# First residuals queued ahead of the third and fourth right factor, and the last quarter finished and stored in two halves

## The chip, the cores and the metric

The kernel runs on one core of one Trainium2 chip. The metric is the device time of one execution in microseconds (us); lower is better. Every time below comes from the kernel's runs or from the trace of one profiled execution.

The core's engines run side by side and meet only at semaphores: TensorE (PE in the profile, its weight loads PEld), VectorE (DVE), ScalarE (ACT) and GpSimd (POOL). SyncE (SP) only issues transfers here. ACT and POOL can issue transfers too. Each engine works through its own instructions in order; an instruction that waits holds back everything behind it on that engine.

## The reference, cut to what matters

`x` has 64 sequences of 64 heads with 1024 features each. All of it is float32.

```python
y   = ssm_conv(x, itok, log_dt, C, ...)       # per head a causal convolution, cut at each sequence's length
s   = y @ Wr.T                                # 64 scores per token (a token is a sequence and a head)
G   = softmax over the 16 highest scores, 0 elsewhere
h   = einsum('nd,krd->nkr', y, A)             # 64 experts of rank 16: 1024 hidden values per token
out = x + 2 * einsum('nkr,kdr->nd', h * G[:, :, None], B)
```

Seen by TensorE, the last two lines are two products of a 1024 x 1024 matrix with 4096 tokens of 1024 values, with a gate between them and the residual `x` added at the end.

## The kernel before, in words

**Tiling.** The 64 heads are cut into 8 groups of 8 heads; with 64 sequences a group has 512 tokens, and its two halves have 256 each (`HT`). A matrix of 1024 features is 8 blocks of 128 partitions.

**First stage (up to 654.3 us).** For each group the convolution (`conv`), the gates (`gates`, `spread_gates`) and the first product (`first`, `seven`) run interleaved. The first product is cut into 2 x 2 blocks and made with seven block products in place of eight. The seven right factors are `y`'s blocks and sums of them; three of those sums stand in tiles of the pool `tq` (called `ty` in the trace). The gated result is written to memory as `hg_dram`, again as the seven right factors that the second product wants. The tile pools `gp`, `tq` and `hp` belong to this stage and are closed before `second` begins.

**Second stage (`second`, from 654.3 us).** It is cut by seven at two levels. The outer list `todo` has 28 entries `(sg, n)`: a pair `sg` of groups, and the outer product `n` in the order 1, 6, 7, 2, 5, 4, 3. The index in this list is `q`. Each entry makes seven inner products with `product(i)` in the order 1, 6, 7, 2, 5, 4, 3. `product(2, c11)` continues to sum in the accumulation bank (PSUM) of `product(1)`, and `product(3, c12)` in that of `product(5)`. Each inner product is two row halves (`ii`) of two matmuls each; in the trace a matmul of float32 counts as two, so that a product is eight rows of 128x256.

- `load_factor(sg, n, halves)` queues the right factor of an entry on SP, 512 KB for each of two groups. `places(q)` says where it goes: for `q % 4` of 2 and 3 it is the tile `qy`, which takes the room of one of the two `y` tiles of the first stage.
- `second_sums` (line 782) makes four sums out of a right factor on DVE (L788 in the trace). `second_level` (line 764) does the same to the left factor the first time that it is used (L771).
- `residuals(sg, m, s)` queues four tiles `o` of `x` on SP, 256 KB each, for one quarter of the output. The pools `op` that hold them lie where `gp`, `tq` and `hp` were.
- `parts_of(sg, n)` says what happens to the inner products. `ahead` and `early` give work on SBUF alone to POOL (`gt_`, line 811, L812 in the trace); `late` adds a bank to its place on DVE (`bank_into`, line 825, and `tt`, L307). `A` is the accumulator `acc_a`. For `n == 6` `ahead` adds the four quarters of `A` to the four tiles `o` of the first residuals, then `early` changes `A` itself.
- `stored` queues the finished 256 KB tile of a quarter on SP (`queued`).

The order on SP is the order in which it is written (`queued` keeps it). The order on DVE and PE is the framework's, by its own estimates, within what is pinned. In `second`, before the loop, the kernel before queues the right factors of `q` 2 and 3 and then the first residuals:

```python
for q in (2, 3):
    r_of[q] = places(q)
    load_factor(*todo[q], r_of[q])
residuals(0, 0, 0)
```

Of the kernel before, what the change touches and what calls it, by code (L numbers as in the profile page):

```python
# [55 lines left out]
NG = NH // HG  # L56
# [4 lines left out]
HT = TOK // NS2  # L61
# [31 lines left out]
def body(ctx: ExitStack, tc, x, xo, lens, par, dvec, at, bm, wt, cst, out):  # L93
    nc = tc.nc
# [266 lines left out]
    s, q = parts  # L361
# [432 lines left out]
    def second(places, rooms, loaded, next_loaded, made, second_level_of, spare, pools):  # L794

        op, ps, A, B = pools
        todo = [(sg, n) for sg in range(NG // 2) for n in (1, 6, 7, 2, 5, 4, 3)]
        outs, loads = {}, [0]  # L800

        def residuals(sg, m, s):
            room = op[loads[0] % len(op)]
            loads[0] += 1
            for a in range(2):
                for gg in range(2):
                    o = room.tile([P, 2, HT], F32, tag="o", name=f"o_{sg}_{m}{s}{a}{gg}")
                    queued(o.rearrange("p i t -> p (i t)"), xo[2 * sg + gg, m, s, a])
                    outs[m, s, a, gg] = o

        def gt_(o, a, b, op_):
            tc.keep_in_program_order(G.tensor_tensor(out=o, in0=a, in1=b, op=op_))  # L812

        PLACES = ((0, 0), (1, 1), (1, 0), (0, 1))
        SIGN = {(0, 0): 1, (0, 1): 1, (1, 0): 1, (1, 1): -1}
        LEFT = {(0, 1): 1, (1, 0): -1, (1, 1): -1}

        def add(engine, o, a, b, plus):
            engine(o, a, b, ALU.add if plus > 0 else ALU.subtract)

        def left_into(o, a, place, v, sign):

            add(gt_, o, a, v, sign * LEFT[place])

        def bank_into(o, place, bank, sign):
            add(tt, o, o, bank, sign * SIGN[place])

        def whole(o, place, bank, v):
            if place == (0, 0):
                nc.scalar.copy(o, bank)  # L830
            elif place == (1, 1):
                stt(o, v, -1.0, ALU.mult, bank, ALU.subtract)
            else:
                add(tt, o, bank, v, LEFT[place])

        def parts_of(sg, n):


            def nothing(*_):
                pass  # L840

            def into(o, sign):
                def early(place, v):
                    left_into(o[place], o[place], place, v, sign)

                def late(place, bank, v):
                    bank_into(o[place], place, bank, sign)
                return early, late

            def out_(m, s):  # L850
                return {p: outs[(m, s) + p] for p in PLACES}

            def stored(m, s, late):
                o = out_(m, s)

                def late_(place, bank, v):
                    late(place, bank, v)
                    queued(out[(2 * sg + place[1], m, s, place[0])],
                           o[place].rearrange("p i t -> p (i t)"))
                return late_  # L860

            def all_of(o, a, op_):
                def ahead():
                    for p in PLACES:
                        gt_(o[p], o[p], a[p], op_)
                return ahead

            if n == 1:
                return nothing, nothing, lambda place, bank, v: whole(A[place], place, bank, v)
            if n == 6:  # L870
                return (all_of(out_(0, 0), A, ALU.add),) + into(A, -1)
            if n == 2:
                early, late = into(out_(0, 0), 1)
                return all_of(out_(1, 1), B, ALU.subtract), early, stored(0, 0, late)
            if n == 7:
                def early(place, v):
                    left_into(B[place], A[place], place, v, 1)

                def late(place, bank, v):
                    add(tt, B[place], A[place] if v is None else B[place], bank, SIGN[place])  # L880
                return nothing, early, late
            if n == 5:
                o = out_(1, 1)

                def late(place, bank, v):
                    if v is None:
                        bank_into(A[place], place, bank, 1)
                        bank_into(o[place], place, bank, -1)
                    else:
                        m = spare[2 if place == (1, 0) else 5]  # L890
                        whole(m, place, bank, v)
                        gt_(A[place], A[place], m, ALU.add)
                        tt(o[place], o[place], m, ALU.subtract)
                return all_of(out_(1, 0), B, ALU.subtract), nothing, stored(1, 1, late)
            m, s = (1, 0) if n == 4 else (0, 1)
            early, late = into(out_(m, s), 1)
            return all_of(out_(0, 1), A, ALU.add) if n == 3 else nothing, early, stored(m, s, late)


        behind = {1: (1, 1), 6: (1, 0), 2: (0, 1)}  # L900
        sums, r_of = {0: loaded}, {1: next_loaded}
        for q in (2, 3):
            r_of[q] = places(q)
            load_factor(*todo[q], r_of[q])
        residuals(0, 0, 0)
        _, *now = parts_of(*todo[0])
        for q, (sg, n) in enumerate(todo):
            if q + 1 < len(todo):
                steps = second_sums(r_of.pop(q + 1), *rooms(q + 1))
            else:  # L910
                steps = iter(())

            def ahead_step():
                next(later, None)
                try:
                    next(steps)
                except StopIteration as e:
                    if e.value is not None:
                        sums[q + 1] = e.value

            right_ = sums.pop(q)
            left_ = made[n]
            early, late = now
            later = second_level_of(todo[q + 3][1]) if q + 3 < 7 else iter(())

            def product(i, bank=None, more=False):
                first = bank is None
                if first:
                    banks, t = (ps, "ps") if more else (ps_f, "pf")
                    bank = banks.tile([P, 2, HT], F32, tag=t, name=f"s{sg}_{n}_{i}")  # L930
                for ii in range(2):
                    for k in range(2):
                        nc.tensor.matmul(  # L933
                            bank[:, ii, :], lhsT=left_[i - 1][:, k, ii * P : (ii + 1) * P],
                            rhs=right_[i - 1][:, k, :],
                            start=(first and ii == 0 and k == 0),
                            stop=(ii == 1 and k == 1 and not more),
                            skip_group_check=True,
                        )
                return bank  # L940

            def new(t, i):
                return fp.tile([P, 2, HT], F32, tag=t, name=f"{t}{i}_{sg}_{n}")

            c11 = product(1, more=True)
            p1 = new("p", 1)
            nc.scalar.copy(p1, c11)  # L947
            p6 = product(6)
            v2 = new("u2", 2)
            tt(v2, p1, p6, ALU.subtract)  # L950
            early((0, 1), v2)
            ahead_step()
            p7 = product(7)
            v3 = new("u3", 3)
            tt(v3, p7, v2, ALU.add)
            early((1, 1), v3)
            early((1, 0), v3)
            if q == 0:
                sum_factors()
            product(2, c11)  # L960
            late((0, 0), c11, None)
            ahead_step()
            c12 = product(5, more=True)
            late((1, 1), c12, v3)
            ahead_step()
            p4 = product(4)
            late((1, 0), p4, v3)
            ahead_step()
            product(3, c12)
            late((0, 1), c12, v2)  # L970
            ahead_step()
            if q + 1 < len(todo):
                ahead, *now = parts_of(*todo[q + 1])
                ahead()
            if n in behind:
                residuals(sg, *behind[n])
            elif n == 4 and sg + 1 < NG // 2:
                residuals(sg + 1, 0, 0)
            if q + 4 < len(todo):
                r_of[q + 4] = places(q + 4)  # L980
                load_factor(*todo[q + 4], r_of[q + 4])
# [90 lines left out]
    for _ in products:  # L1072
# [3 lines left out]
        if n in (5, 6):  # L1076
            i = (1, 6)[n - 5]
# [77 lines left out]
```

## Time and profile before

| | us |
|---|---|
| three runs | 1003.79, 1004.41, 1004.69 (median 1004.41) |
| profiled execution, its own time | 1004.42 |
| its span in the trace | 1002.6 |
| time outside the span | 1.82 |
| PE busy | 985.1 (98% of the span) |
| DVE busy | 717.5 (72%) |
| POOL busy | 330.8 (33%) |
| ACT busy | 165.8 (17%) |
| mean DMA rate | 140 GB/s |

A timeline row has the start in us, the duration in us, the engine, the line, the operation, the tile written and the tiles read, the shape and the count. Rows of equal work that follow each other are merged. A bracket gives the idle time before the row and what ended it. PE's rows overlap by about 0.17 us, since a matmul's end is modelled. In the answers on waits, a row has who waited, for whom, the total in us, the number of waits and the longest. PEclk is the TensorE clock that was granted, as a share of full speed.

### The profile page before, as it was taken

To read this page: it belongs to the slowest core of one execution; us is meant where nothing else is said; L and a number is where in the kernel's file an instruction comes from. 1 tells how busy PE (TensorE), PEld (TensorE's weight loads), DVE (VectorE), ACT (ScalarE), POOL (GpSimd) and SP (SyncE) were. 2 spreads that over 40 slices of the span, in tenths; PEclk is the share of its full clock that TensorE was granted. 3 is DMA by queue.
4 is the path that set the end of the run, shared out by engine and by line. 5 is a ranking of instruction groups with operands and counts; after the bars stand their busy time and mean duration, and the time that the engine had idled before them with its cause. 6 is when DMAs were issued, how large, how long until landed. Compare 5 with 4: busy or idle time off the path is not lost.

```text
span 1002.6 us, 12158 instructions
## 1 busy us (share of the span) xinstructions
PE 985.1 (98%) x4416; PEld 738.4 (74%) x4416; DVE 717.5 (72%) x1672; ACT 165.8 (17%) x339; POOL 330.8 (33%) x278
## 2 busy tenths in 40 slices
PE   7999999999999999999999999998999999999998
PEld 3367666686676676677677578887888888888887
DVE  6887778587587587676646649778965786686674
ACT  5436041131141041031001100000000000000000
POOL 0002023122123113114103202245655673654555
PEclk9999999999999999999999999999999999999999
DMA  7113316315405315315315154473474367267432
GB/s 273 64 53 112 126 42 184 137 52 154 137 22 184 118 40 163 137 43 163 115 65 158 48 198 163 158 272 137 158 264 167 126 211 271 85 210 253 132 119 105
DMA packets 66189, 140.86 MB, mean 140 GB/s; under 512 B 9362, under 2 KB 17874, under 8 KB 66130
## 3 DMA queue, kind: packets, MB, share of 16 engines
q1 hardware_dynamic: 49376, 94.54, 27.4%
q0 software_dynamic: 15744, 44.07, 14.0%
q10 hardware_dynamic: 1010, 1.48, 0.6%
q8 instruction: 35, 0.57, 0.2%
q14 instruction: 24, 0.20, 0.1%
HBM read 92.79 MB, written 47.25 MB: 140 GB/s over the span
## 4 chain that ended last, share of the span: by engine, by line
PE 96%; DVE 3%; DMA 1%; issue 0%; SPq 0%; DVEq 0%
PE h L502 38%; PE s L933 33%; PE pc L581 6%; PE pc L587 5%; PE pu L555 5%; PE psh L640 3%; PE sum L190 2%; PE pb L277 1%; DMA waa<-in_at 1%; PE psc L649 1%; PE pb L279 1%; DVE t L788 0%; DVE y L593 0%; PE pg L685 0%; PE pk L292 0%
## 5 line engine op out<-in xcount | busy, mean ns | idle before, releaser
L318 DVE SCALAR_TENSOR_TENSOR s<-s,turn 128x64 f32<-128x64 f32 (+1 forms) x576 | 146.0, 303 | 36.7 <-ACT s L560 30.2
L502 PE MATMUL h<-y,waa 128*128 128x256 f32 x512 | 122.7, 384 | 0.0
L502 PE MATMUL h<-y,was 128*128 128x256 f32 x512 | 117.8, 381 | 0.0
L502 PE MATMUL h<-ty,was 128*128 128x256 f32 x512 | 116.4, 380 | 0.0
L502 PEld LDWEIGHTS h<-y,waa 128*128 128x128 f32 x512 | 93.7, 190 | 27.0 <-issue 15.4
L502 PEld LDWEIGHTS h<-y,was 128*128 128x128 f32 x512 | 96.1, 190 | 19.9 <-issue 7.5
L502 PEld LDWEIGHTS h<-ty,was 128*128 128x128 f32 x512 | 96.6, 190 | 16.7 <-issue 3.9
L719 POOL TENSOR_TENSOR hg<-h_p,gx 128x512 f32<-128x512 f32 x16 | 26.8, 1678 | 223.1 <-DVE h_p L318 215.4
L719 POOL TENSOR_TENSOR hg<-h_u,gx 128x512 f32<-128x512 f32 x32 | 49.5, 1546 | 136.2 <-DVE h_u L307 136.1
L593 DVE TENSOR_TENSOR y<-pc,mask 128x512 f32<-128x512 f32 x64 | 42.5, 684 | 37.0 <-PE pc L587 37.0
L947 ACT COPY p<-s 128x512 f32<-128x512 f32 x28 | 16.4, 586 | 317.4 <-PE s L933 317.4
L696 POOL DMA_DIRECT2D gx<-gt_dram x56 | 33.5, 625 | 97.2 <-DMA gt_dram<-gt 90.3
L812 POOL TENSOR_TENSOR o<-o,acc_a 128x512 f32<-128x512 f32 x32 | 48.5, 1535 | 47.8 <-ACT acc_a L830 21.7
L581 PE MATMUL pc<-x,toep 128*128 128x512 f32 x128 | 62.0, 607 | 0.0
L502 PE MATMUL h<-ty,waa 128*128 128x256 f32 x256 | 58.8, 382 | 0.0
L307 DVE TENSOR_TENSOR hg<-hg 128x512 f32<-128x512 f32 x64 | 42.8, 689 | 21.4 <-POOL hg L719 20.5
L560 ACT COPY s<-pu 128x448 f32<-128x448 f32 x64 | 33.9, 532 | 140.8 <-PE pu L555 140.4
L587 PE MATMUL pc<-s,w 64*128 64x448 f32 x256 | 56.8, 562 | 0.0
L502 PEld LDWEIGHTS h<-ty,waa 128*128 128x128 f32 x256 | 47.9, 190 | 10.7 <-issue 4.6
L555 PE MATMUL pu<-x,bt 128*64 128x448 f32 x256 | 55.5, 553 | 0.0
L812 POOL TENSOR_TENSOR o<-o,b_room 128x512 f32<-128x512 f32 x32 | 49.9, 1580 | 9.8 <-DVE b_room L307 9.8
L307 DVE TENSOR_TENSOR o<-o,s 128x512 f32<-128x512 f32 x52 | 35.4, 681 | 23.6 <-PE s L933 18.5
(225 smaller groups left out, 1627.8 us busy)
## 6 DMA issues: line engine op xcount, KB each, us to landing
x<-in_x SPq DMA_DIRECT2D x32, 512.0 KB
hg_dram<-hg POOLq DMA_DIRECT2D x16, 1024.0 KB, 6.0
o<-in_xo SPq DMA_DIRECT2D x64, 256.0 KB
out<-o SPq DMA_DIRECT2D x64, 256.0 KB
gx<-gt_dram POOLq DMA_DIRECT2D x56, 256.0 KB, 6.6
qy<-hg_dram SPq DMA_DIRECT2D x28, 512.0 KB
r<-hg_dram SPq DMA_DIRECT2D x26, 512.0 KB
hg_dram<-hg POOLq DMA_DIRECT2D x16, 768.0 KB, 4.4
```

Source lines behind the costliest of these rows:

```text
L307: V.tensor_tensor(out=o, in0=a, in1=b, op=o_)
L318: V.scalar_tensor_tensor(out=o, in0=a, scalar=s, in1=b, op0=o1, op1=o2)
L502: nc.tensor.matmul(bank[:, ii, :], lhsT=fac[n - 1][:, k, (j + ii) * P : (j + ii + 1) * P], rhs=rf[n - 1][:, k, :], start=(first and ii == ...
L555: nc.tensor.matmul(pu[hh * NS : (hh + 1) * NS, :], lhsT=bt[:, i, (1 - c) * P + hh * NS : (1 - c) * P + (hh + 1) * NS], rhs=xt[:, hh, : NCH ...
L560: nc.scalar.copy(s[:, c], pu.rearrange("p (k b) -> p k b", b=NB))
L581: nc.tensor.matmul(pc, lhsT=toep[:, 2 * i + hh, :], rhs=xt[:, hh, :], start=True, stop=False)
L587: nc.tensor.matmul(pcs[hh][:, NB:], lhsT=w[o : o + NS, c, i, 1:], rhs=s[o : o + NS, c].rearrange("p k b -> p (k b)"), start=False, stop=(c ...
L593: marks["y"] = V.tensor_tensor(out=y[:, :, :, 2 * i + hh, :], in0=pcs[hh].rearrange("p (k s b) -> p k s b", s=NS2, b=HB), in1=mask.rearran ...
L696: i = queue.dma_start(gx[:, ii, :], gt_dram[g, c * n : (c + 1) * n, :].unsqueeze(1).to_broadcast([n, RANK, TOK]),)
L719: G.tensor_tensor(out=o, in0=a, in1=b, op=op)
L812: tc.keep_in_program_order(G.tensor_tensor(out=o, in0=a, in1=b, op=op_))
L933: nc.tensor.matmul(bank[:, ii, :], lhsT=left_[i - 1][:, k, ii * P : (ii + 1) * P], rhs=right_[i - 1][:, k, :], start=(first and ii == 0 an ...
```

## The change

The first residuals are queued ahead of the right factors of `q` 2 and 3. And in the last entry of the list, the last inner product is made by its two row halves: each is added to its half of the output tile and stored by itself, the first half through SP, the second through ACT's queue.

```diff
+        def last_out(product, bank):
+            sg, o = NG // 2 - 1, outs[0, 1, 0, 1]
+            for ii in range(2):
+                product(3, bank, rows=(ii,))
+                bank_into(o[:, ii], (0, 1), bank[:, ii], 1)
+                (queued, scalar_queued)[ii](
+                    out[2 * sg + 1, 0, 1, 0][:, ii * HT : (ii + 1) * HT], o[:, ii])
+
+        def scalar_queued(o, i):
+            tc.keep_in_program_order(nc.scalar.dma_start(o, i))
...
+        residuals(0, 0, 0)
         for q in (2, 3):
             r_of[q] = places(q)
             load_factor(*todo[q], r_of[q])
-        residuals(0, 0, 0)
...
-            def product(i, bank=None, more=False):
+            def product(i, bank=None, more=False, rows=(0, 1)):
...
-                for ii in range(2):
+                for ii in rows:
...
-            product(3, c12)
-            late((0, 1), c12, v2)
+            if q + 1 < len(todo):
+                product(3, c12)
+                late((0, 1), c12, v2)
+            else:
+                last_out(product, c12)
```

## The prediction

> **What bounds the kernel now.** I read the page's chain of work first, then PE's waits from 640 us on, then the timeline around the one large wait, then SP's issues and the DMA rate ahead of it, and last the final 6 us. The chain that ended last:
>
> ```profile
> PE 96%; DVE 3%; DMA 1%; issue 0%; SPq 0%; DVEq 0%
> ```
>
> PE sets the end, so only what PE waits for, and what follows its last matmul, is worth anything. In the second stage PE waited twice:
>
> ```profile
> PE s L933 <- DVE acc_a L307: 3.2, 1, 3.2
> PE s L933 <- DVE o L307: 0.4, 1, 0.4
> ```
>
> From entry 4 on (708.56) to the last product (996.92) PE makes 167 products in 288.36 us, 1.727 each, with no gap. By that step the second product of entry 2, fifteen after 654.32, was due at 680.22. It starts at 685.40: **5.18 us are lost in entry 1**, and another 0.71 in entry 3. The timeline of the first:
>
> ```profile
> 665.87 1.26 POOL L812 TENSOR_TENSOR o<-o,acc_a 128x512 f32<-128x512 f32 x1 [3.17 <-DMA o<-in_xo]
> ...
> 670.13 0.69 DVE L307 TENSOR_TENSOR u<-p,s 128x512 f32<-128x512 f32 x1 [0.91 <-PE s L933]
> ...
> 670.51 4.61 POOL L812 TENSOR_TENSOR o<-o,acc_a 128x512 f32<-128x512 f32 x3 [3.38 <-DMA o<-in_xo]
> 670.74 1.58 DVE L771 TENSOR_TENSOR e<-wbs 128x512 f32<-128x512 f32 x1
> ...
> 675.20 5.05 POOL L812 TENSOR_TENSOR acc_a<-acc_a,u 128x512 f32<-128x512 f32 x3
> ...
> 675.72 1.75 DVE L788 TENSOR_TENSOR t<-qy 128x512 f32<-128x512 f32 x1
> ...
> 677.50 1.64 DVE L788 TENSOR_TENSOR t<-qy,t 128x512 f32<-128x512 f32 x1
> 679.06 1.74 DVE L788 TENSOR_TENSOR qy<-qy 128x512 f32<-128x512 f32 x1
> 680.73 0.67 DVE L307 TENSOR_TENSOR acc_a<-acc_a,s 128x512 f32<-128x512 f32 x1
> ...
> 681.46 3.46 PE L933 MATMUL s<-b_room,ey 128*128 128x256 f32 x8 [3.23 <-DVE acc_a L307]
> ...
> 684.71 0.86 PE L933 MATMUL s<-qy,wbs 128*128 128x256 f32 x2
> 685.40 1.89 PE L933 MATMUL s<-ey,e 128*128 128x256 f32 x8
> ```
>
> Read backwards: `product(3, c12)` may not write its bank before DVE has read it (680.73). That read stands in DVE's order behind three sums of `qy`, stretched from 0.68 to 1.7 us by POOL. POOL is late because its four adds into the first residuals waited for those to land, at 665.8 and 670.5. Of the 5.18 us, 3.23 are idle time and 1.78 slow matmuls: the next ten rows take 3.94 us, not 2.16. SP's issues, and the DMA share and GB/s (the last two columns) ahead of that:
>
> ```profile
> 644.15 0.80 SPq L776 DMA_DIRECT2D b_room<-hg_dram  x2
> 654.51 1.75 SPq L776 DMA_DIRECT2D qy<-hg_dram  x4
> 656.30 15.67 SPq L776 DMA_DIRECT2D o<-in_xo  x8
> ```
>
> ```profile
> 652.00:654.00 2.00, 2.00 (x11) 1.77 (x10) 1.97 (x3) 0.00 (x0) 1.53 (x1) 1.00 0.00 0
> ...
> 658.00:660.00 2.00, 2.00 (x11) 1.77 (x10) 1.93 (x4) 0.00 (x0) 0.55 (x1) 1.00 1.07 416
> ```
>
> The DMA engines stand idle until 655.3 because SP waits for PE's last use of `y`, whose room `qy` takes; then they are full, and the residuals are last in line. The end:
>
> ```profile
> 996.92 1.89 PE L933 MATMUL s<-qy,e 128*128 128x256 f32 x8
> ...
> 998.85 0.69 DVE L307 TENSOR_TENSOR o<-o,s 128x512 f32<-128x512 f32 x1 [0.98 <-PE s L933]
> ```
>
> DVE ends at 999.54; the store and the end of the program take 3.06 us more.
>
> **What the Trainium skill says.** (1) "SBUF — State Buffer", section "SBUF: two separate sides": a DVE operation with two SBUF inputs and a POOL operation that reads SBUF exclude each other for the whole instruction. The trace agrees to 0.1 us: POOL 1.26 alone, DVE 0.68 alone, but 1.6 to 1.75 where they meet, while DVE operations that read a bank stay at 0.68 beside a busy POOL. (2) "TensorE: Matmul & The Clock Gate", section "Part 1: The HAM clock gate": after an idle window of about 3.4 us TensorE runs at half clock until a busy window has passed. The trace agrees: PEclk 0.50 from 682 to 685 after 3.23 us idle; after a gap of 1.38 us before 55.87 it was not (1.00). (3) "PSUM — Partial Sum Buffer", section "PSUM bank collisions raise a hardware error": accesses must be kept apart by bank, not by address. That bears on the split tail.
>
> **Part 1: residuals first.** Moved on SP: four issues of 256 KB past four of 512 KB. Nothing is added or removed. In the built program the first residual waits only for the inner product that reads `tq`'s last sum, the last but one of the first stage, done at 651.0; `qy` keeps its own wait (654.5). So:
> - Residuals: issue 651.1, data 0.8 us later (as `qy`: 654.51 to 655.3), 1.05 MB at 416 GB/s 2.5 us, completion at most 1.5 (as at the end of the trace): landed by about 655.9. Had they waited as long as `qy`, 659.3, which would still do.
> - `qy`: 0 to 2.5 us later than before, where its first sum ran at 667.21. With the 0.79 MB store of `hg` in between, 3.9 MB at 416 from 655.3 is 664.7, with completion 666. First use is now 671.35. Hidden. The second `hg` store and the loads behind it gain from the idle time used.
> - POOL's four adds then wait for ACT and DVE alone: after POOL's store issue (ends 662.7) they run 662.7 to 668.7, beside DVE work that reads banks. Before they ended at 675.1.
>
> The built order on DVE also changes: in entry 1 the sums of `qy` are spread between the other work. Three sums of `qy` leave the free stretch from 667.2 to 669.2 and come after `u`; between `u` (670.13) and the bank read that PE needs there are six sums with two SBUF inputs, as before, but beside them POOL has three adds where it had six. I walk it with the lock rule: DVE alone 0.60 a step back to back, after POOL its end + 0.57; POOL 1.13 once it has the lock. On the old order this gives 672.3, 674.0, 677.5, 679.1 and 680.8 for the stretched sums' ends, as the trace has. New order: u 670.82; e 671.42; POOL `acc_a` 672.55; ey 673.12; u3 673.73; ey 674.33; POOL 675.46; qy 676.03; POOL 677.16; meanwhile `acc_a` (first bank) 676.63; e 677.73; t 678.33; **`acc_a` (the wanted bank) 678.93**. PE goes on at 679.0 in place of the due 676.77: 2.23 us lost, not 5.18. After it DVE catches up by 683.7, ahead of the next bank at 684.4, and from there order and distances are those of before, the 0.71 of entry 3 included. **Gain 2.95.** Bounds: no lock at all, acc_a at 676.6, all 5.18; three POOL operations each in full (3.4) and the clock gated again (1.8), about 0.
>
> **Part 2: the tail.** Two matmul halves, two DVE adds of 128x256 (0.42 each, as the gate rows of that shape) in place of one of 0.69, two stores of 128 KB. The built program makes the second half's first matmul wait for DVE's read of the first half: same bank. So: first half issued by 997.78, DVE 0.20 later to 998.40, PE again 0.06 later (as 681.40 to 681.46), 0.86 to 999.32, DVE 999.52 to 999.94: 0.40 later than 999.54. The store has half the bytes (0.67 us at 390 GB/s): -0.33. ACT's issue takes longer to move data (603.38 to 604.45, 1.07; SP 0.84): +0.2. **Cost 0.3**, between -0.4 (no wait on the bank) and +0.7 (no saving in the store). SP's and POOL's last work is done by then; nothing queues behind.
>
> **Sum.** Against the profiled execution's own 1004.42 (span 1002.6 and 1.82 around it): -2.95 + 0.3 = -2.65, **1001.8 us**. The median of the runs, 1004.41, is the same. About 0.2% (2 us) is what a measurement of this kernel can tell from no change.
>
> **Rivals.**
> - *PE's wait goes entirely* (0.15): POOL's adds fall beside DVE's bank reads and the read is done by 676.7. For: its four residual adds are gone from the crowded stretch. Against: three POOL adds, started by `u` and `u3`, remain there. 1004.42 - 5.18 + 0.3 = 999.5.
> - *The clock is gated although the wait is shorter* (0.24): the gap is 2.2 us, between the 1.38 that was harmless and the 3.23 that was not, and where the windows fall is chance. 1.8 of the gain is lost: 1003.6, no change by the bound.
> - *`qy` lands late* (0.06), ending slower: 1 MB is now ahead of it, and DVE's sums of it stand ahead of the read that frees PE. Up to 672.0 POOL's lock hides it; past that each us costs PE one, so that landing at 675 eats the gain, and past 677 it is slower by 2 us. At 678.5 the wait is 8.2 us and the clock gated (1.8): 10.0 - 5.18 + 0.3, about 1009.5. Against: 666 by the sum above, 5 us early.
>
> **Numbers.** The likeliest case (0.55) is 1001.8, its own range 1001.1 to 1002.4 by 0.6 us of lock order and tail. Down to 999.4 lies the first rival, up to 1003.7 most of the second: range 999.4 to 1003.7. Faster 0.70 (first case and first rival), same 0.24, slower 0.06.
>
> **What would show it.** Right: POOL's first residual add begins near 662.7, four in a row, with no wait for a DMA; PE's wait on `acc_a` is about 2.2 us and PEclk stays at 1.00; the 0.4 us wait on `o` is still there; a new PE wait of about 0.6 us on DVE near the end, and the span's last 3.06 us shorter by little. Wrong: DVE waiting for `qy`, PEclk of 0.50 near 680, or a PE wait above 3 us.

## The result, and the profile after

| | before | changed |
|---|---|---|
| median of 13 runs each, us | 1004.41 (1002.83 to 1004.98) | 1001.48 (1001.00 to 1002.44) |
| profiled execution, its own time | 1004.42 | 1001.41 |
| its span | 1002.6 | 999.6 |
| start of the second stage | 654.32 | 654.05 |
| lost in entry 1 | 5.18 | 2.23 |
| second stage's start to the span's end | 348.3 | 345.55 |

The ratio is 0.9973, 95% interval 0.9966 to 0.9981: faster by 2.9 us (0.3%), with 1001.8 forecast. "Lost in entry 1" is worked out as in the prediction: the start of the second product of entry 2, less the second stage's start and 15 products of 1.727 us. For the changed kernel that is 682.18 - (654.05 + 25.90) = 2.23.

The chain that ended last, from the changed kernel's page, in shares of the span:

```profile
PE 94%; DVE 3%; DMA 2%; issue 1%; SPq 0%; POOL 0%; DVEq 0%; POOLq 0%
```

PE still sets the end. Its waits in the changed kernel from 640 us on (who waited, for whom, total, times, longest):

```profile
PE s L945 <- DVE acc_a L307: 2.0, 1, 2.0
PE s L945 <- DVE o L307: 1.0, 2, 0.5
```

The large wait went from 3.2 to 2.0 us. The waits on `o` are now two: the one of entry 3 is still there, and the tail has one of its own. SP's issues and the timeline of entry 1 in the changed kernel:

```profile
650.79 1.76 SPq L776 DMA_DIRECT2D o<-in_xo  x4
...
654.24 1.75 SPq L776 DMA_DIRECT2D qy<-hg_dram  x4
...
662.44 2.51 POOL L812 TENSOR_TENSOR o<-o,acc_a 128x512 f32<-128x512 f32 x2
...
665.38 1.27 POOL L812 TENSOR_TENSOR o<-o,acc_a 128x512 f32<-128x512 f32 x1 [0.43 <-DVE acc_a L307]
...
667.11 1.27 POOL L812 TENSOR_TENSOR o<-o,acc_a 128x512 f32<-128x512 f32 x1 [0.46 <-DVE acc_a L307]
...
669.86 0.69 DVE L307 TENSOR_TENSOR u<-p,s 128x512 f32<-128x512 f32 x1 [2.83 <-PE s L945]
...
670.69 1.58 POOL L812 TENSOR_TENSOR acc_a<-acc_a,u 128x512 f32<-128x512 f32 x1 [2.32 <-DVE u L307]
671.06 1.76 DVE L788 TENSOR_TENSOR ey<-qy 128x512 f32<-128x512 f32 x1
...
673.50 3.32 POOL L812 TENSOR_TENSOR acc_a<-acc_a,u 128x512 f32<-128x512 f32 x2 [1.23 <-DVE u L307]
673.94 1.75 DVE L788 TENSOR_TENSOR qy<-qy 128x512 f32<-128x512 f32 x1
...
676.21 1.16 DVE L771 TENSOR_TENSOR e<-wbs,e 128x512 f32<-128x512 f32 x1
...
677.90 0.68 DVE L307 TENSOR_TENSOR acc_a<-acc_a,s 128x512 f32<-128x512 f32 x1
...
678.62 1.99 PE L945 MATMUL s<-b_room,ey 128*128 128x256 f32 x8 [1.97 <-DVE acc_a L307]
...
682.18 1.89 PE L945 MATMUL s<-ey,e 128*128 128x256 f32 x8
```

Read it against the timeline of before. The residuals are issued 3.5 us ahead of `qy`, while the DMA engines had stood idle. No POOL row waits for a DMA any more: the four adds into the residuals are done at 668.38, where they ended at 675.12. What is left beside DVE's sums are POOL's three adds into `acc_a`, and each of them still makes one DVE sum long (1.76, 1.75, 1.16, where 0.68 is alone). The read that frees PE ends at 678.58 in place of 681.40.

PE's own order in this place changed too, which no edit asked for. The row ahead of the wait, from the timeline of before and from that of the changed kernel:

```profile
676.77 1.46 PE L933 MATMUL s<-qy,wbs 128*128 128x256 f32 x6
```

```profile
674.77 1.89 PE L945 MATMUL s<-t,wbs 128*128 128x256 f32 x8
```

Before, six of the eight rows of entry 2's first product ran ahead of the product that waits; now none does. So PE asks for its bank 1.3 us sooner, and the idle time fell by 1.26 us only, though the read ends 2.55 us sooner after the second stage's start. With the six rows still ahead some 1.3 us of the wait would have been covered; that is an estimate from these two timelines, and no run holds PE's order.

The granted clock after the shorter wait, in the changed kernel's stretches of 2 us (the third number from the right is PEclk):

```profile
678.00:680.00 2.00, 1.38 (x6) 1.00 1.06 416
680.00:682.00 2.00, 2.00 (x11) 1.00 0.72 293
```

It stays at 1.00, so the 1.78 us of slow matmuls that followed the wait before are gone too, but for 0.10 that the first product after the wait takes longer than usual (1.99 us in place of 1.89). That is the larger part of the gain: of the 2.95 us, 1.26 are the shorter idle time and about 1.7 the clock. In all 13 runs the changed kernel's mean clock is 0.999 or 1.0, where the profiled execution of before has 0.998. The tail of the changed kernel:

```profile
993.69 1.03 PE L945 MATMUL s<-qy,e 128*128 128x256 f32 x4
993.95 1.23 DVE L307 TENSOR_TENSOR o<-o,s 128x512 f32<-128x512 f32 x2 [1.04 <-PE s L945]
...
995.23 1.13 PE L945 MATMUL s<-qy,e 128*128 128x256 f32 x4 [0.51 <-DVE o L307]
...
996.40 0.42 DVE L307 TENSOR_TENSOR o<-o,s 128x256 f32<-128x256 f32 x1 [1.22 <-PE s L945]
996.90 0.36 ACTq L909 DMA_DIRECT2D out<-o  x1
```

The merged DVE row holds the read of the bank before and the read of the first half; PE's second half waits 0.51 us for the latter.

### The profile page after: what moved, and what is told of

The parts are those of the page before. It is cut to its first block, busy times and chain, and to the rows that moved or that the text cites. A ratio compares the mean times of both kernels' runs of the same rounds, so it can differ in the third digit from the quotient of the medians.

```text
span 999.6 us, 12169 instructions
## 1 busy us (share of the span) xinstructions
PE 983.3 (98%) x4416; PEld 737.0 (74%) x4416; DVE 716.2 (72%) x1673; ACT 166.0 (17%) x339; POOL 330.2 (33%) x278
## 4 chain that ended last, share of the span: by engine, by line
PE 94%; DVE 3%; DMA 2%; issue 1%; SPq 0%; POOL 0%; DVEq 0%; POOLq 0%
PE h L502 38%; PE s L945 32%; PE pc L581 6%; PE pc L587 5%; PE pu L555 5%; PE psh L640 3%; PE sum L190 2%; PE pb L277 1%; DMA waa<-in_at 1%; DMA hg_dram<-hg 1%; PE psc L649 1%; PE pb L279 1%; DMA o<-in_xo 1%; DVE y L593 0%; PE pg L685 0%
## 5 line engine op out<-in xcount | busy, mean ns | idle before, releaser
L307 DVE TENSOR_TENSOR o<-o,s 128x512 f32<-128x512 f32 (+1 forms) x53 | 35.6, 672 | 23.9 <-PE s L945 18.1
```

The lines of the kernel that those rows point to most:

```text
L307: V.tensor_tensor(out=o, in0=a, in1=b, op=o_)
```

## The experiments

The theory: PE's wait is set by the order in which DVE and POOL get a lock, one instruction at a time; taking POOL's four residual adds out of the way takes 1.26 of the 3.23 us of waiting and the slow clock after it, POOL's three other adds keep the rest, and the tail costs a little. The rivals: the order of DVE's instructions, which the change moved too, brings the gain; the remaining wait is the length of DVE's queue and not POOL's lock; the tail is part of the gain.

The experiments ran in three sets, each on one chip with the kernel before beside it, at medians of 1004.91 (experiments 1 to 4), 1004.55 (5, 6, the first run of 7, and 8) and 1004.61 us (the second run of 7, and 9). The first stage, which is the same in all of them, ended between 652.96 and 655.50 in the profiled executions. So the table counts each profiled execution from its second stage's start, which takes that difference out.

| kernel | median us | ratio to before (95%) | stage 2 starts | lost in entry 1 | start of stage 2 to span's end |
|---|---|---|---|---|---|
| before | 1004.41 | | 654.32 | 5.18 | 348.3 |
| changed | 1001.48 | 0.9973 (0.9966 to 0.9981) | 654.05 | 2.23 | 345.55 |
| residuals first alone | 1001.92 | 0.997 (0.9959 to 0.9981) | 654.25 | 2.24 | 345.35 |
| tail alone | 1004.37 | 0.9996 (0.9988 to 1.0004) | 654.68 | 5.39 | 348.7 |
| changed, last 5/3 in two banks | 1001.00 | 0.9962 (0.995 to 0.9975) | 654.43 | 2.24 | 344.8 |
| changed, entry 1 by hand | 999.10 | 0.9943 (0.993 to 0.9957) | 654.00 | 0.00 | 343.3 |
| before with DVE's new order | 1007.49 | 1.003 (1.0018 to 1.0042) | 655.50 | 3.43 | 349.5 |
| changed without the early adds | 1000.15 | 0.9957 (0.9944 to 0.9971) | 655.45 | 0.00 | 343.35 |
| both remedies | 999.27 | 0.9947 (0.9934 to 0.9959) | 654.94 | 0.00 | 342.55 |
| both remedies again | 998.57 | 0.9947 (0.9933 to 0.996) | 654.12 | 0.00 | 342.6 |
| entries 1, 2, 3 by hand | 1003.37 | 0.9987 (0.998 to 0.9994) | 654.80 | 0.00 | 346.4 |
| both, read of entry 3 first | 999.02 | 0.995 (0.9937 to 0.9962) | 654.41 | 0.00 | 342.7 |
| both, one sum of entry 3 later | 998.87 | 0.9944 (0.9932 to 0.9957) | 652.96 | 0.00 | 342.65 |

**1. Residuals first alone.** Part 1 of the change without part 2:

```diff
+        residuals(0, 0, 0)
         for q in (2, 3):
             r_of[q] = places(q)
             load_factor(*todo[q], r_of[q])
-        residuals(0, 0, 0)
```

> Part 1 alone: the kernel before with the four residual loads queued ahead of qy's, and the old tail. Theory (POOL's four residual adds were late and stood in VectorE's way; the tail is a small cost): the whole gain and no tail cost, so about 2.95 us under before (1001.4) and some 0.2 us under the changed kernel; PE's wait on acc_a near 678 is 2.0 us as in the changed kernel, PEclk 1.00, and from the start of the last inner product to the end of the span it is 5.7 us as before. Rival (the tail brings part of the gain): it stays a few tenths of a us over the changed kernel, and with the tail's share large over 1002.5.

Measured: the whole gain. The same 1.97 us wait on `acc_a`, 2.24 us lost in entry 1, and from the second stage's start 345.35 us, 0.2 less than the changed kernel; 5.68 of them follow the last product's start, as before. The median is 2.99 us under that of before beside it, where the changed kernel's is 2.93 under its own.

**2. Tail alone.** The kernel before with `last_out` (part 2 of the diff), the residuals queued last.

> Part 2 alone: the kernel before, with only the last inner product made and stored in two halves. Theory: PE's wait on acc_a stays at 3.2 us with PEclk 0.50 after it; from the start of the last inner product to the end of the span 5.9 us against 5.7 before, so 0.2 us slower than before (1004.6), which the runs cannot tell from no change. Rival (the split hides half of the add and of the store): 0.5 us or more shorter at the end, about 1003.9.

Measured: no difference that its interval can tell from none. PE's large wait is the old one, and so is the slow clock after it (a timeline row, and two stretches of 1 us with PEclk third from the right):

```profile
682.02 3.65 PE L945 MATMUL s<-b_room,ey 128*128 128x256 f32 x8 [3.44 <-DVE acc_a L307]
```

```profile
683.00:684.00 1.00, 1.00 (x4) 0.50 0.52 209
684.00:685.00 1.00, 1.00 (x3) 0.50 0.11 45
```

The two runs settle where the gain sits: all of it in part 1. The tail is worth about 0.2 us of loss in the traces (5.9 us from the last product's start to the span's end, where before has 5.7), too little for the medians to show: this kernel's is 0.5 us under that of before beside it, and 3 of its 13 executions had a mean clock of 1.0, so that they may have missed the slow stretch.

**3. The tail's two halves in two banks.** The changed kernel, with the product 5 that the last product continues made in one bank for each row half:

```diff
-            c12 = product(5, more=True)
-            late((1, 1), c12, v3)
+            if q + 1 < len(todo):
+                c12 = product(5, more=True)
+                late((1, 1), c12, v3)
+            else:
+                c12 = [product(5, more=True, rows=(ii,)) for ii in range(2)]
+                o = outs[0, 1, 1, 1]
+                for ii in range(2):
+                    bank_into(o[:, ii], (1, 1), c12[ii][:, ii], 1)
+                queued(out[2 * sg + 1, 0, 1, 1], o.rearrange("p i t -> p (i t)"))
...
-                            start=(first and ii == 0 and k == 0),
-                            stop=(ii == 1 and k == 1 and not more),
+                            start=(first and ii == rows[0] and k == 0),
+                            stop=(ii == rows[-1] and k == 1 and not more),
...
-                product(3, bank, rows=(ii,))
-                bank_into(o[:, ii], (0, 1), bank[:, ii], 1)
+                product(3, bank[ii], rows=(ii,))
+                bank_into(o[:, ii], (0, 1), bank[ii][:, ii], 1)
```

> The changed kernel, with the last entry's fifth and third inner product in two accumulation banks, one for each row half (the add of the fifth is split in two as well). Theory (the split tail costs because the second half's matmuls wait for VectorE's read of the first half, same bank): the wait of 0.5 us is gone, the last add of 128x256 ends 0.8 us sooner after the start of the last inner product, 5.1 us in place of 5.9 to the end of the span, about 0.8 us under the changed kernel (1000.7). Rival (the cost is in the second store's queue or its size): the wait goes, but the end of the span stays at 5.7 us or more from that start.

Measured: PE's last eight rows run without a gap, and DVE's last add follows at once (timeline of this kernel):

```profile
994.09 1.89 PE L945 MATMUL s<-qy,e 128*128 128x256 f32 x8
994.35 1.23 DVE L307 TENSOR_TENSOR o<-o,s 128x512 f32<-128x512 f32 x2 [1.36 <-PE s L945]
996.02 0.42 DVE L307 TENSOR_TENSOR o<-o,s 128x256 f32<-128x256 f32 x1 [0.44 <-PE s L945]
```

From the last product's start to the span's end it is 5.1 us, 0.8 less than the changed kernel and 0.57 less than before, so the split does pay once the halves have a bank each. What cost it its worth is the shared bank: PE's second half waited there for DVE's read of the first.

**4. DVE's order of entry 1 by hand.** The changed kernel with three of `qy`'s sums pinned ahead of `u`, in the stretch where DVE had waited 2.83 us for PE (the bracket of the `u` row at 669.86 above). The whole of DVE's order in entry 1 is then the written one:

```diff
-                steps = second_sums(r_of.pop(q + 1), *rooms(q + 1))
+                steps = second_sums(r_of.pop(q + 1), *rooms(q + 1), q == 1)
...
+            by_hand = ExitStack()
+            if q == 1:
+                by_hand.enter_context(tc.manual_schedule(engines={V.engine}))
+                for _ in range(3):
+                    next(steps)
...
+            by_hand.close()
```

> The changed kernel, with VectorE's order in entry 1 written out by hand: three sums of qy before u, in the stretch where VectorE is idle, and only three sums with two SBUF inputs between u and the bank read that PE waits for (six in the changed kernel). Theory (what is left of the wait is VectorE's work ahead of that read, stretched by the lock with POOL): by the walk with the lock the read ends at 676.3 on the clock of the profile of before, ahead of the due 676.77, so PE does not wait at all in entry 1, another 2.2 us are gained, about 999.4. Rival (the load of qy or POOL's adds set the read): PE still waits 1 us or more on acc_a, or VectorE waits for qy ahead of u.

Measured: PE's wait on `acc_a` is gone. The rows of this kernel's timeline:

```profile
667.06 1.65 POOL L812 TENSOR_TENSOR o<-o,acc_a 128x512 f32<-128x512 f32 x1 [0.46 <-DVE acc_a L307]
667.61 1.65 DVE L788 TENSOR_TENSOR ey<-qy,ey 128x512 f32<-128x512 f32 x1
...
671.01 1.76 DVE L788 TENSOR_TENSOR t<-qy,ey 128x512 f32<-128x512 f32 x1
...
673.89 1.38 DVE L771 TENSOR_TENSOR e<-wbs,e 128x512 f32<-128x512 f32 x1
...
675.19 0.67 DVE L307 TENSOR_TENSOR acc_a<-acc_a,s 128x512 f32<-128x512 f32 x1
...
676.44 1.03 PE L950 MATMUL s<-qy,wbs 128*128 128x256 f32 x4
677.31 1.89 PE L950 MATMUL s<-b_room,ey 128*128 128x256 f32 x8
```

Sums still collide: `ey` (1.65 us) ahead of `u`, where nobody waits for it, and `t` (1.76) and `e` (1.38) between `u` and the wanted read. But three sums stand in that stretch in place of six, so the read ends at 675.86, ahead of the product at 677.31 that needs its bank. So the remaining 2.2 us were not a limit of the engines; they hung on how many sums stood in POOL's stretch. This run alone doesn't tell the lock from the mere number of sums; experiment 6 bears on that.

**5. The new order without the early residuals.** The changed kernel's DVE order in entry 1 differs from before's. This run gives the kernel before that order, its residuals still queued last. To hold the order of entry 1, that of entry 2 is written out as well:

```diff
+            if q in (1, 2):
+                by_hand.enter_context(tc.manual_schedule(engines={V.engine}))
...
+            if q == 1:
+                for _ in range(2):
+                    next(steps)
             product(2, c11)
```

> The kernel before, its residuals still queued last, but with DVE's order of entries 1 and 2 written out by hand, so that entry 1 has the changed kernel's order: u, two sums, u3, a sum, a sum of qy, the first read into acc_a, two sums, the wanted read. Lock theory (the gain needs POOL's four adds early, and the order alone brings nothing): POOL's adds still wait for the residuals' landing near 670.5, the walk with the lock puts the wanted read's end at 681.4, PE waits 3.2 to 4.5 us on acc_a, the clock is mostly gated after it, and the time is 1004.4 to 1005.7. Rival (the order of DVE brings the gain, the residuals only cause it): PE waits about 2 us, 1001.5 to 1002.

The total missed what both theories gave. Where it went is in this kernel's timeline:

```profile
671.28 4.63 POOL L812 TENSOR_TENSOR o<-o,acc_a 128x512 f32<-128x512 f32 x3 [2.99 <-DMA o<-in_xo]
...
681.40 0.67 DVE L307 TENSOR_TENSOR acc_a<-acc_a,s 128x512 f32<-128x512 f32 x1
...
682.13 1.99 PE L936 MATMUL s<-b_room,ey 128*128 128x256 f32 x8 [3.16 <-DVE acc_a L307]
...
694.61 1.99 PE L936 MATMUL s<-qy,e 128*128 128x256 f32 x8 [0.99 <-DVE b_room L307]
...
709.15 1.99 PE L936 MATMUL s<-qy,e 128*128 128x256 f32 x8 [2.19 <-DVE o L307]
```

In entry 1 it is nearly as the lock theory said: POOL still waits for the residuals, and PE waits 3.16 us on `acc_a` where before waited 3.23; the rival's 2 us are not there. Counted from the second stage's start, the wanted read ends after 27.08 us before, 26.57 in this run and 24.53 in the changed kernel. So the order alone brings 0.5 of the 2.55 us, and the rest came only with the residuals early. The other half of the pair, early residuals with the old order, was not run.

The 3.43 us lost in entry 1, with 5.18 before, are no gain of the order: the wait is all but the same, and this profiled execution kept the full clock after it, which makes all but 0.07 of the difference of 1.75. (Three of the five executions had a mean clock of 0.996 or 0.998.) So the slow clock alone costs about 1.7 us here.

The total has other losses. PE waits 0.99 us in entry 2, where the written order puts sums of 1.37 and 1.75 us ahead of the read that frees PE, and 2.19 in entry 3, where it was 0.45 before. Neither belongs to entry 1's order: the changed kernel has the same order there, leaves entry 2 to the framework, and waits only the 0.44 in entry 3. And the first stage ended 1.2 us later than in the profile of before. So the order alone doesn't bring the gain; on the total this run says nothing.

**6. POOL's three early adds left out.** This part of the sum is not computed; DVE's order is the changed kernel's:

```diff
-                return (all_of(out_(0, 0), A, ALU.add),) + into(A, -1)
+                early, late = into(A, -1)
+                return all_of(out_(0, 0), A, ALU.add), early if sg else nothing, late
```

> The changed kernel without POOL's three early adds into acc_a in entry 1 of the first pair, so that this part of the sum is left out; DVE's order is that of the changed kernel. Lock theory (the 2 us that remain are the lock's: each of POOL's three adds holds DVE for over a us): with them gone DVE's sums run at 0.6 to 0.7 us, the wanted read ends near 676.3 and PE doesn't wait in entry 1; 2.2 us less than the changed kernel, 999.1 to 999.5. Rival (the read is late for the count of DVE instructions ahead of it, whatever POOL does): the wait on acc_a stays near 2 us, 1001.5.

Measured: the same sums in the same places, now short, and no wait of PE on `acc_a` (timeline of this kernel):

```profile
672.47 0.68 DVE L788 TENSOR_TENSOR ey<-qy 128x512 f32<-128x512 f32 x1
...
674.27 0.68 DVE L788 TENSOR_TENSOR qy<-qy 128x512 f32<-128x512 f32 x1
...
676.68 0.68 DVE L307 TENSOR_TENSOR acc_a<-acc_a,s 128x512 f32<-128x512 f32 x1
...
677.90 1.89 PE L946 MATMUL s<-b_room,ey 128*128 128x256 f32 x8
```

Nothing is lost in entry 1: the wanted read ends 21.91 us after the second stage's start, with 24.53 in the changed kernel. The median, 1000.15, is above the expected 999.1 to 999.5; the profiled execution of 1000.57 had its second stage start at 655.45, 1.4 us later than the changed kernel's. Counted from there it is 2.2 us shorter than the changed kernel, as expected. So the number of DVE instructions ahead of the read doesn't make the wait by itself: as many without POOL's adds don't (this run), and fewer beside POOL's adds don't either (experiment 4). Here it needs both, six sums and POOL's three adds in the same stretch.

**7. Both remedies.** Experiments 3 and 4 together, run on two chips.

> The changed kernel with both remedies: DVE's order of entry 1 by hand with three sums of qy ahead of u, and the last entry's product 5/3 in two banks, one for each row half. If the two losses are apart from each other, their gains add: 2.3 us for the wait on acc_a and 0.5 to 0.8 for the tail, 998.3 to 998.7, with only the 0.4 us wait on o in entry 3 left. If the hand order had also hidden part of the tail's cost, no less than 999.1.

> The kernel with both remedies once more, on the chip of the two runs beside it, since the first stage differs by up to 1 us between calls: measured from the stage's start nothing is lost in entry 1, 0.71 in entry 3, and the time is 998.3 to 999.3.

Measured: 999.27 the first time, outside what adding had given and on the other branch's side of 999.1, and 998.57 the second time. The total can't decide here. From the second stage's start both are 342.6 us, 0.7 less than entry 1 by hand alone, against 0.8 that two banks had brought. The gains add; the difference between the two runs lies in the first stage (654.94 and 654.12). This kernel takes 0.9947 of before's time (0.9933 to 0.996), and from the second stage's start it is 3 us shorter than the changed kernel.

**8. Entries 1, 2 and 3 by hand.** As experiment 7 with `if q in (1, 2, 3)` in the condition for the hand order.

> As the run with both remedies, but with DVE's order by hand in entries 1, 2 and 3, so that entry 3 keeps its four sums of the next right factor behind the work that the banks wait for. It aims at the 0.71 us lost in entry 3 to the wait on o. If that wait comes from the sums placed ahead of the read by the framework, it goes, and the time is 0.7 less than with both remedies: 997.6 to 998.0. If it comes from POOL's lock alone, the wait stays at 0.4 to 0.5 and the time is the same; if the sums are then late for the next entry, a new PE wait of up to 0.7 us shows at its start.

A miss for every branch: 1003.37. PE's waits in this kernel from 640 us on:

```profile
PE s L951 <- DVE o L307: 2.4, 2, 2.2
PE s L951 <- DVE b_room L307: 1.0, 1, 1.0
```

They have the places and sizes of the two waits that experiment 5 had. In entry 2 the cause is the same written order. In entry 3 the sums no longer stand ahead of `u`, and two of them (`ey`, 1.75 us each) meet POOL's adds ahead of the wanted read. From the second stage's start it is 3.85 us longer than both remedies; about 0.7 of them are lost behind entry 3.

**9. Entry 3, two cuts.** Both keep the framework's order in entry 2 and write out entries 1 and 3. The first puts a left-factor sum (L771) behind the wanted read; the second moves one sum of the next right factor (`t`) from ahead of `u` to behind the first left-factor sum. The diff below has both edits in one; its remarks say which line is whose:

```diff
+            if q in (1, 3):
+                by_hand.enter_context(tc.manual_schedule(engines={V.engine}))
+                for _ in range(3 if q == 1 else 4):     # second cut: 3 in both
+                    next(steps)
...
             late((0, 0), c11, None)
-            ahead_step()
+            if q != 3:                                  # first cut only
+                ahead_step()
...
             ahead_step()
+            if q == 3:                                  # first cut only
+                ahead_step()
             p4 = product(4)
```

> As the run with both remedies, and in entry 3 DVE's order by hand too: the four sums of the next right factor stay ahead of u, but the second left-factor sum (L771) stands behind the wanted read of the bank of product 5 instead of ahead of it. Lock theory: that sum has two SBUF inputs, met POOL's second add and took 1.79 us; with it gone the read needs only POOL's add into the same tile, which ends near 46.0 us after the stage's start, so it ends near 46.9 where 47.2 was, and PE loses 0.1 to 0.4 us in entry 3 in place of 0.71: 0.3 to 0.6 less than with both remedies. Rival (the read is late because of what stands ahead of u): 0.71 stays.

> As the run with both remedies, and in entry 3 by hand one sum of the next right factor (t) moved from ahead of u to behind the first left-factor sum. Rival of the lock theory (sums ahead of u delay the chain, so fewer of them help): u starts 0.5 to 1.7 us earlier and the 0.71 us of entry 3 go. Lock theory: the number of sums with two SBUF inputs ahead of the wanted read is unchanged, but both now fall beside POOL's adds, which u starts; by the walk the read ends 0.4 us later and entry 3 loses 1.1 us, so 0.4 more than with both remedies.

The loss is read at the first product of entry 4, due 28 products (48.36 us) after the stage's start. Both remedies: 703.18 - 654.12 - 48.36 = 0.70. First cut: 703.05 - 654.41 - 48.36 = 0.28, as expected. But the time from the stage's start, 342.7, is that of both remedies. The first cut's timeline shows why:

```profile
701.22 1.99 PE L951 MATMUL s<-qy,e 128*128 128x256 f32 x8
...
725.23 0.69 DVE L307 TENSOR_TENSOR o<-o,s 128x512 f32<-128x512 f32 x1 [1.29 <-POOL o L812]
...
725.97 1.99 PE L951 MATMUL s<-r,e 128*128 128x256 f32 x8 [0.24 <-DVE o L307]
```

The wait of entry 3 is gone and a new one stands in entry 5, where POOL's adds into `o` are late for DVE. The gain is given back there. In the second cut `u` starts 40.7 us after the stage's start in place of 42.4, and yet entry 3 loses 0.79 us: an earlier `u` doesn't help. That is 0.09 more than both remedies, where the walk gave 0.4 more: the walk has the direction here and misses the size by 0.3 us.

## Why the prediction was right

**What bounds.** 5.18 us were lost in entry 1 before; experiments 4 and 6 show that all of the remaining 2.23 can go, by moving three of DVE's sums or by leaving out POOL's three adds.

**Part 1, the transfers.** The residuals are issued at 650.79 (651.1 was forecast, less the 0.27 by which this execution's second stage starts earlier: 650.83). POOL's first add is at 662.44 (662.7 less 0.27 is 662.43). One detail differed: the four do not follow in a row, the last two wait 0.43 and 0.46 us for DVE's `acc_a`; they end at 668.38, with 668.7 less 0.27 forecast. When the transfers landed was not measured, only that nobody waited for them: the residuals by 662.44 (forecast 655.9), and `qy` by 666.89, where its first sum starts in experiment 4 (forecast 666).

**Part 1, the walk.** Shifted by those 0.27 us, the forecast ends were: POOL's first `acc_a` 672.28, `ey` 672.85, `qy` 675.76, the wanted read 678.66. The trace has 672.27, 672.82, 675.69 and 678.58. A walk with three constants (0.60 a DVE step, 0.57 after POOL's release, 1.13 for POOL) held to 0.1 us over eight microseconds. That the loss is 2.23 us to the digit is luck: PE went on at 678.62, 0.11 sooner than forecast, and its first product then took 0.10 us longer than the step of 1.727, which the sum left out. The walk also rests on PE's order in the built program, which is why it could start from a due time of 676.77; the prediction doesn't say that this order was new. The Trainium skill, "SBUF — State Buffer", section "SBUF: two separate sides", says that the port pair is locked for a whole instruction and not shared: experiment 6 agrees most directly, since the same sum takes 1.76 us beside a POOL add and 0.68 without it. So the opening's sentence that the engines meet only at semaphores is too strong: DVE and POOL meet here as well, in instructions that share no tile.

**The rivals.** That the wait goes entirely would have needed POOL's adds beside DVE's bank reads; three sums were still caught, as argued. The clock was not gated after 1.97 us in the profiled execution, and no mean clock of the 13 runs is under 0.999. The prediction had this as a matter of odds (0.24 for the slow clock), and 1.8 of its 2.95 us hung on it: here it had luck as well as the right mechanism. `qy` was in no engine's wait.

**Part 2.** Forecast +0.3, measured +0.23 (5.91 us from the last product's start to the span's end, 5.68 before), out of two terms that were each a little off. PE's second half starts 1.54 us after the first, as forecast, but DVE's last add ends 0.51 us later than before and not 0.40: the first rows after the wait take 0.10 us longer (1.13 for the four rows in place of 1.03), which the sum left out. And after DVE's end it is 2.78 us, where 3.06 - 0.33 + 0.2 = 2.93 was forecast. The two misses nearly cancel. The lower bound of -0.4, for no wait on the bank, was too high: experiment 3 measured -0.57. The mechanism, PE held by a read of the same bank, is shown by experiment 3. The rule itself is in the Trainium skill, "PSUM — Partial Sum Buffer", section "PSUM bank collisions raise a hardware error": keep accesses apart by bank. No run here breaks it, so what would happen otherwise isn't shown.

**The sum.** -2.65 was forecast against the profiled 1004.42. Measured is -3.01: the 2.95 of entry 1 less 0.23 for the tail, and 0.27 for a first stage that ended earlier by chance. The last is no part of the change. So the forecast is right by its terms: 2.95 and 0.3 forecast, 2.95 and 0.23 measured.

## What to carry to other kernels

When an idle DMA queue has something behind a transfer that must wait, let the one that can go now go first; but count what then remains on the engines, since here the transfer was only the first of two causes. Price the clock apart from the wait: here it was more than half of the gain. On a pair of engines that lock each other out, a sum's place decides what it costs: put it where nobody waits, and walk the lock by hand, because an instruction taken from one collision may meet the next. Before splitting a tail, see that the halves don't share a bank, or the split buys a wait for what it saves.

## What the runs showed of the hardware that was not expected

- Whether the slow clock follows a wait of about 3.2 us isn't settled by its length, as far as these runs go. After 3.16 us of idle PE in experiment 5 PEclk stayed at 1.00; after 3.23 (before) and 3.44 (experiment 2) it was 0.50 for about 3 us; after 1.97 it was 1.00. The Trainium skill, "TensorE: Matmul & The Clock Gate", section "Part 1: The HAM clock gate", gives a free-running window of about 3.4 us. 3.23 us are less than that, but only by about the 0.17 us by which PE's rows overlap in these traces, so they don't contradict it. Of the 53 runs of the kernel before beside the experiments, 51 had a mean clock of 0.997 or 0.998 and two had 1.0 (1003.36 and 1003.59 us); of the 13 of experiment 2, three had 1.0. That these escaped the slow clock of entry 1 fits, but their traces were not taken. Nor is a shorter wait shown to be safe: 9 of the 21 executions of experiment 8 had a mean clock of 0.998, though its trace has no wait over 2.20 us in the second stage and the full clock after it. Where their slow stretch lies is open.
- The first stage, with the same instructions, ended anywhere from 652.96 to 655.50 us in the profiled executions. That is as much as most of the edits here are worth, and is why they are compared from the second stage's start.
